# Halved patch loads with a matrix step between them, in a four-layer convolution network on one Trainium2 core

## The chip, the core and the metric

The kernel runs on one core of a Trainium2 chip. A core has TensorE (PE, matrix products into PSUM), VectorE (DVE), ScalarE (ACT), GpSimd (POOL) and SyncE (SP), which here does nothing but issue DMAs; sixteen DMA engines move data between HBM and SBUF. The metric is the device time of one execution in microseconds (us), the median of a few runs.

## What is computed

x is 16 images of 64 x 64 positions and 256 channels in float32, and everything stays float32. Four layers follow each other, each as x = x + f(groupnorm(x)) with 32 groups:

```
layer 0: linear attention with 8 heads over the 4096 positions, out projection, layer norm
layer 1: channel gate, two maps (mean, max over channels), 7x7 convolution of them -> fac,
         a state scan over the 4096 positions (16 states) added to fac,
         x * gate * fac, then batch norm over all 16 images, relu
layer 2: involution 3x3: per position 16 x 9 weights from a small network, applied to a projection
layer 3: involution 7x7: per position 16 x 49 weights from a small network, applied to groupnorm(x)
```

The batch norm of layer 1 needs a mean and a variance per channel over all images, so all of x1 * fac has to be seen once before its first value can be used.

## The kernel before

`network` is one program of four stages, with DRAM tensors between them: `x1_d` (layer 0's result), `fac_d` (fac, one row of 512 positions for each image and eighth of an image), `x2_d`, `x3_d` and `c3_d` (layers 1 and 2), and `strips` (layer 2's result, centred, cut in strips of 14 columns for the 7x7 patches, four quarters of 64 channels).

**Scan** (lines 631 to 780). For every eighth of the positions (`ch`) and each half of the images (`g`), `rowed` transposes the three rows of each of the 16 images (delta, delta times m squared, delta times m) to 48 partitions of `rows` (L726, L731). `decayed` (L733) makes two products of 48 partitions by 512 positions (L736), one for the decay, with an exponential on ACT (L740), and one for the input. A scan instruction on DVE follows (L749), four small products (L760), and two small DVE instructions (L767, L768). `ch` by `g` are 16 steps, written out in the text's order. At the end fac is transposed to `held`, and stored to `fac_d` (L779).

**Statistics** (L784 to L836). For each of 16 images and 8 eighths, a tile of x1 (512 KB, four buffers) is loaded (L789), PE spreads the row of `held` over the partitions (L792), DVE forms (x1 − mean) * fac with its sum (L797), ACT its squares with their sum (L801); then small DVE instructions make `bnp` and `ab`, the batch norm's factors.

**Layer 2** (L896 on) starts with its constants (L912 to L918: 5 loads, and 10 small ones in `folded`, L849). It is a pipeline of 152 turns, written out under `tc.manual_schedule()`: an image's eighth passes `end_of_layer1` (L960: the product again, L970, relu on ACT, L976, the sum on POOL, L980, and squares, L987), 13 turns later `projected`, from 21 on the involution, and 32 turns later `centred`. `loads(n + 1)` issues a turn's loads one turn ahead; `load_layer1` (L947) loads x1 and a spread copy of fac.

**Layer 3** (L1282 on). A turn is two bands of three rows of one quarter (64 channels) of one image: 16 x 4 x 11 = 704 turns. `load_patches` (L1404) loads a turn's patches `xw`, two DMAs of 128 partitions by 2 KB, six buffers, four turns ahead. `involution7` (L1433) multiplies them with the position's weight matrices, 32 products of 126 partitions, 32 columns and 48 elements (L1442), into a PSUM tile `pa`, from which ACT (L1454), DVE (L1455) and POOL (L1462, with the residual `rx`) make the output. Beside this, `matrices` (L1358) makes the weight matrices `wm` of the next quarter, in 24 steps; a step is four products on 64-row halves (L1376) into one of three PSUM tiles, then four ACT instructions (L1386) or one on DVE (L1391). `STEPS` spreads them: 3, 2, 2, 3, 2, 3, 2, 2, 3, 2 and 0 steps after the products of turns 0 to 10. Every third or fourth turn has a part of the next image's `reduced` (L1343). The last image's strips are made here, in eight units that borrow buffers of `xw` (L1515 to L1529).

The order of an engine's instructions is the text's inside `tc.manual_schedule()`, which holds for the scan and layer 2; elsewhere, layer 3 included, a scheduler may move them. All DMAs are issued by SP, in order, on eight semaphores in rotation: a DMA waits until the one eight before it has landed. A pool's tile waits for the release of the tile that had the buffer before. Every float32 product is two weight loads and two matmul records on PE.

The lines of layer 3's loop that the prediction needs:

```python
            if n + 4 < len(turns):
                pats.append(load_patches(*turns[n + 4]))
            ...
            involution7(i, quarter, t, wms[i, quarter], msk, pats.pop(0), ex[:, t % 2], rx[:, t % 2])
            ...
            for _ in range(STEPS[t]):
                next(making, None)
```

Of the kernel before, what the change touches and what calls it, by code (L numbers as in the profile page):

```python
# [15 lines left out]
P = 128  # L16
# [20 lines left out]
def network(ctx: ExitStack, tc: tile.TileContext, a: dict, out: bass.AP):  # L37
# [593 lines left out]
    with ExitStack() as st:  # L631
# [4 lines left out]
        sm = st.enter_context(tc.tile_pool(name="s_sm", bufs=2, space=PSUM))  # L636

# [6 lines left out]
        bng = sconst("bng", [P, 2], a["bn_gamma"])  # L644
        bnb = sconst("bnb", [P, 2], a["bn_beta"])
# [4 lines left out]
        wrow = sconst("wrow", [3 * NI, NG, 2, P], a["wrow"].rearrange("k (g n s) -> k g n s", g=NG, n=2))  # L650
        wout = sconst("wout", [P, 16], a["wstate"])
        mv2 = sconst("mv2", [P, 2, 2, NI])
# [56 lines left out]
        r3 = sconst("r3", [P, NB, NI, 3])  # L709
        rd, rdmm, rdm = (r3[:, :, :, k].rearrange("p d i -> p i d") for k in range(3))  # L710
        nc.vector.scalar_tensor_tensor(rd, z, 0.0, az, ALU.max, ALU.add)
        nc.vector.tensor_tensor(rdm, rd, m, ALU.mult)
        nc.vector.tensor_tensor(rdmm, rdm, m, ALU.mult)
# [5 lines left out]
        with tc.manual_schedule():  # L719
# [3 lines left out]
            def rowed(ch):  # L723
                pr = tr.tile([P, CT], F32, tag="tr", name="pr")
                for q in range(4):
                    nc.tensor.transpose(  # L726
                        pr[0 : 3 * NI, q * P : (q + 1) * P],
                        r3[:, ch * 4 + q].rearrange("p i k -> p (i k)"), ident,
                    )
                rows[ch] = wk.tile([3 * NI, CT], F32, tag="rows", name="rows", bufs=2)  # L730
                nc.scalar.copy(rows[ch], pr[0 : 3 * NI, :])  # L731

            def decayed(ch, g):  # L733
                pa = mm.tile([P, 2, CT], F32, tag="mm", name="pa")
                for k in range(2):
                    nc.tensor.matmul(  # L736
                        pa[:, k], lhsT=wrow[:, g, k, :], rhs=rows[ch], start=True, stop=True
                    )
                da = wk.tile([P, CT], F32, tag="da", name="da")
                nc.scalar.activation(da, pa[:, 0], AF.Exp)  # L740
                ins[ch, g] = da, pa
# [38 lines left out]
        facr = fac_d.rearrange("(i c) t -> i (c t)", i=NI)  # L780
# [3 lines left out]
        tot = sconst("tot", [P, 2, 2, NI, NCH])  # L784
        for i in range(NI):
            for ch in range(NCH):
                tk = slice(ch * CT, (ch + 1) * CT)
                x1 = wk.tile([P, 2, CT], F32, tag="x1", name="x1", bufs=4)
                nc.sync.dma_start(out=x1, in_=x1_d[i, :, :, tk].rearrange("h p t -> p h t"))  # L789
                pf = tr.tile([P, CT], F32, tag="tr", name="pf")  # L790
                row = i * NCH + ch
                nc.tensor.matmul(  # L792
                    pf, lhsT=ident[0:n, row : row + 1].broadcast_to([n, P]), rhs=held[0:n],
                    start=True, stop=True,
                )
                for h in range(2):
                    nc.vector.scalar_tensor_tensor(  # L797
                        x1[:, h], x1[:, h], ngm1[:, i, h : h + 1], pf, ALU.add, ALU.mult,
                        accum_out=tot[:, 0, h, i, ch : ch + 1],
                    )  # L800
                    nc.scalar.activation(  # L801
                        x1[:, h], x1[:, h], AF.Square, accum_out=tot[:, 1, h, i, ch : ch + 1]
                    )
        for k in range(2):
            nc.vector.tensor_reduce(mv2[:, :, k, :], tot[:, k], AX.X, ALU.add)
        nc.vector.tensor_scalar(mv2, mv2, 1.0 / NT, None, ALU.mult)
        sqm = sconst("sqm", [P, 2, NI])
        nc.vector.tensor_tensor(sqm, mv2[:, :, 0, :], mv2[:, :, 0, :], ALU.mult)
        nc.vector.tensor_tensor(mv2[:, :, 1, :], mv2[:, :, 1, :], sqm, ALU.subtract)
        for h in range(2):  # L810
            gate = ab[:, 0, :, h]
            nc.vector.tensor_tensor(mv2[:, h, 0], mv2[:, h, 0], gate, ALU.mult)
            nc.vector.tensor_tensor(mv2[:, h, 1], mv2[:, h, 1], gate, ALU.mult)
            nc.vector.tensor_tensor(mv2[:, h, 1], mv2[:, h, 1], gate, ALU.mult)


        mvb = sconst("mvb", [P, 2, 2])
        nc.vector.tensor_reduce(mvb[:, 0, :], mv2[:, :, 0, :], AX.X, ALU.add)
        nc.vector.tensor_scalar(mvb[:, 0, :], mvb[:, 0, :], 1.0 / NI, None, ALU.mult)
        dev = mv2[:, :, 0, :]  # L820
        for h in range(2):
            nc.vector.tensor_scalar(dev[:, h], dev[:, h], mvb[:, 0, h : h + 1], None, ALU.subtract)
        nc.vector.tensor_tensor(dev, dev, dev, ALU.mult)
        nc.vector.tensor_tensor(dev, dev, mv2[:, :, 1, :], ALU.add)
        nc.vector.tensor_reduce(mvb[:, 1, :], dev, AX.X, ALU.add)
        nc.vector.tensor_scalar(mvb[:, 1, :], mvb[:, 1, :], 1.0 / NI, None, ALU.mult)
        inv_sqrt(bnp[:, 0, :], mvb[:, 1, :], BN1_EPS)
        nc.vector.tensor_tensor(bnp[:, 0, :], bnp[:, 0, :], bng, ALU.mult)
        nc.vector.tensor_tensor(bnp[:, 1, :], mvb[:, 0, :], bnp[:, 0, :], ALU.mult)
        nc.vector.tensor_tensor(bnp[:, 1, :], bnb, bnp[:, 1, :], ALU.subtract)  # L830
        nc.vector.tensor_tensor(
            ab.rearrange("p t i h -> p (t i) h"),
            ab.rearrange("p t i h -> p (t i) h"),
            bnp[:, 0, :].unsqueeze(1).broadcast_to([P, 2 * NI, 2]),
            ALU.mult,
        )  # L836

    maps_st.close()

# [35 lines left out]
    def centred_strips(i, u, xc, cen, mean):  # L875

        nc.gpsimd.tensor_tensor(
            cen.rearrange("p q t c -> p t q c"),
            xc.rearrange("p t (q c) -> p t q c", q=4),
            mean.rearrange("p (q c) -> p q c", q=4).unsqueeze(1).broadcast_to([P, 4, 4, 64]),  # L880
# [4 lines left out]
        for w, dt in copies:  # L885
            for th in range(2):
                t0, t1 = max(0, th * 4 + dt), min(NTC, th * 4 + 4 + dt)
                s0 = t0 - th * 4 - dt
                parts.append((
                    strips[i, :, 3 : 3 + HW, w, t0:t1, :].rearrange("q r t c -> r q (t c)"),  # L890
                    cen[th:P:2, :, s0 : s0 + t1 - t0, :].rearrange("p q t c -> p q (t c)"),
                ))
# [3 lines left out]
    with ExitStack() as st:  # L896
# [20 lines left out]
        nc.sync.dma_start(out=ws[64:65, :], in_=a["bs"])  # L917
        sb2 = folded(pc, "l2", "L2_mean", "L2_var", "L2_gamma", "L2_beta", "br")  # L918
# [14 lines left out]
        loaded, stores, begun = [], [], []  # L933

# [25 lines left out]
        def end_of_layer1(i, rc):  # L960
# [6 lines left out]
            x1, pf = taken("x1"), taken("pf")  # L967
            zs = [wk.tile([P, 2, 256], F32, tag="z", name="z", bufs=1), pf]
            for h, z in enumerate(zs):
                nc.vector.scalar_tensor_tensor(  # L970
                    z, x1[:, h], ngm1[:, i, h : h + 1], pf, ALU.add, ALU.mult
                )
# [216 lines left out]
        def loads(n):  # L1189
# [6 lines left out]
            if end:  # L1196
                load_layer1(*end)

        with tc.manual_schedule():
            loads(0)  # L1200
# [81 lines left out]
    with ExitStack() as st:  # L1282
# [121 lines left out]
        def load_patches(i, quarter, t):  # L1404

            xw = wk.tile([P, 2, NTC, 64], F32, tag="xw", name="xw", bufs=6)
            rows = strips[i, quarter].rearrange("r w t c -> (r w) (t c)")
            for k in range(2):
                t0 = (t + k * NTT) * TR * (TC + 6)
                nc.sync.dma_start(  # L1410
                    out=xw[:, k].rearrange("p t c -> p (t c)"), in_=rows[t0 : t0 + P]
                )
# [20 lines left out]
        def involution7(i, quarter, t, wm, msk, xw, ex, rx):  # L1433


            pa = sm.tile([P, CT], F32, tag="sm", name="pa")
            pav = pa[:, 0 : 2 * TR * HW].rearrange("c (g a w) -> c (g a) w", g=2, w=HW)
            for tj in range(NTC):
                for k in range(2):
                    for q in range(2):  # L1440
# [5 lines left out]
                            lhsT=xw[0:TILE_IN, k, tj, 32 * q : 32 * q + 32],  # L1446
# [4 lines left out]
                        )  # L1451
            pag = pa[:, 0 : 2 * TR * HW].rearrange("c (g t) -> c g t", g=2)
# [23 lines left out]
        pats = [load_patches(*t) for t in turns[:4]]  # L1476
# [8 lines left out]
        gap = min(44, (4 * NTT * (NI - 1) - 4) // NCH)  # L1485
        for n, (i, quarter, t) in enumerate(turns):
# [21 lines left out]
            if n + 4 < len(turns):  # L1508
                pats.append(load_patches(*turns[n + 4]))
# [5 lines left out]
            if n % gap == 1 and n // gap < NCH:  # L1515
                xc = wk.tile([P, 4, C], F32, tag="xw", name="xc", bufs=6)
                nc.sync.dma_start(out=xc, in_=centred_from(NI - 1, n // gap))
# [8 lines left out]
            involution7(i, quarter, t, wms[i, quarter], msk, pats.pop(0), ex[:, t % 2], rx[:, t % 2])  # L1526
            if n % gap == 2 and n // gap < NCH:
# [130 lines left out]
```

## Time and profile before

| What | Value |
|---|---|
| three runs | 8206.47, 8218.75, 8226.33 us; median 8218.75 |
| profiled execution | 8218.71 us; span from first to last instruction 8216.8 us |
| instructions in the span | 213,294, of which PE 88,348 matmuls and as many weight loads |
| busy in the span | PE 83%, DVE 72%, ACT 59%, POOL 37% |
| DMA | 1695.53 MB, 206 GB/s on average |
| granted TensorE clock | 0.918 on average |
| layer 0 | 0 to 3053 us |
| scan, statistics | to 3174, to 3408 us |
| layer 2 | to about 5840 us |
| layer 3 | to 8214 us |

The profile shows one execution. An instruction group's line has its engine, line of the kernel, operation, tiles written and read and their shapes, and in square brackets how long the engine had been idle before it and which instruction ended the wait; "issue" means that no instruction or DMA of the profile ended it. PEld are weight loads, PE the matmuls. In the view by stretches each engine has its busy us and its count of instructions, and at the end stand the granted clock, the DMA engines' mean busy share and GB/s. DMA queue q1 carries the program's transfers, q8 and q14 carry instructions.

### The profile page before, as it was taken

How to read it: one execution, taken by the hardware profiler on the slowest of the kernel's cores; microseconds unless marked ns; L12 is line 12 of the kernel's file. 1: busy time of each engine (PE TensorE's matmuls, PEld its weight loads, DVE VectorE, ACT ScalarE, POOL GpSimd, SP SyncE). 2: the span in 40 equal slices, each digit the busy share in tenths (PEclk: the TensorE clock that was granted, in tenths of full speed). 3: DMA queues.
4: the chain of work that ended last, by engine and by line, in shares of the span. 5: the costliest groups of instructions: out<-in, count | busy, mean ns of one | idle time of the engine just before them, and what ended most of it. 6: DMA issues, size and time to landing. Idle time of an engine off the chain costs nothing. (4 is left out here: it accounts for less than half of the span.)

```text
span 8216.8 us, 213294 instructions
## 1 busy us (share of the span) xinstructions
PE 6831.6 (83%) x88348; PEld 5191.9 (63%) x88348; DVE 5933.2 (72%) x7071; ACT 4827.7 (59%) x11136; POOL 3044.1 (37%) x2154
## 2 busy tenths in 40 slices
PE   7888888888888867478888888888588888888897
PEld 5666666666666643156666666666477777777776
DVE  6787778787777775679999999999644444444444
ACT  3555555555555544676776767665455555555554
POOL 1222222222222210167888888887411212111112
PEclk9999999999999977798888888888799999999999
DMA  7644444344333334766777777775588888888887
GB/s 225 188 142 138 139 136 141 131 145 144 124 113 118 116 102 151 249 221 231 268 262 261 271 252 267 262 258 200 176 257 258 259 258 256 261 259 257 255 256 245
DMA packets 1079706, 1695.53 MB, mean 206 GB/s; under 512 B 136785, under 2 KB 682914, under 8 KB 1077586
## 3 DMA queue, kind: packets, MB, share of 16 engines
q1 hardware_dynamic: 1078738, 1681.89, 63.1%
q8 instruction: 696, 11.40, 0.6%
q14 instruction: 272, 2.23, 0.1%
HBM read 1234.54 MB, written 469.76 MB: 207 GB/s over the span
## 5 line engine op out<-in xcount | busy, mean ns | idle before, releaser
L1102 DVE TENSOR_TENSOR pd<-xs,pw 128x4608 f32<-128x4608 f32 x256 | 1261.2, 4946 | 1.4 <-ACT xs L1083 1.4
L1376 PE MATMUL pk<-rt,span 64*128 64x176 f32 x12288 | 1177.9, 328 | 52.6 <-issue 47.9
L1386 ACT ACTIVATE wm<-pk,spanb 128x176 f32<-128x176 f32 x2560 | 845.7, 424 | 573.4 <-PE pk L1376 570.3
L1115 POOL TENSOR_TENSOR pd<-pd 128x2048 f32<-128x2048 f32 (+2 forms) x384 | 1071.6, 2791 | 173.1 <-DVE pd L1102 82.7
L1462 POOL TENSOR_TENSOR ex<-ex,rx 128x192 f32<-128x192 f32 (+2 forms) x768 | 436.6, 570 | 1820.6 <-DVE ex L1455 1232.1
L1376 PEld LDWEIGHTS pk<-rt,span 64*128 64x128 f32 x12288 | 967.8, 191 | 132.8 <-issue 75.9
L1455 DVE SCALAR_TENSOR_TENSOR ex<-pa,msk,ex 128x192 f32<-128x192 f32 x704 | 294.3, 418 | 1006.5 <-ACT ex L1454 948.4
L292 PE MATMUL pkv<-wq,xn 128*128 128x256 f32 x4096 | 967.9, 382 | 14.4 <-ACT va L301 14.2
L1442 PE MATMUL pa<-wm,xw 126*32 126x48 f32 x45056 | 758.2, 214 | 220.9 <-issue 206.2
L375 POOL TENSOR_TENSOR qa<-qa,mq 128x1024 f32<-128x1024 f32 x256 | 507.4, 2005 | 1168.8 <-DVE mq L384 503.0
L1079 PE MATMUL pt<-ident,pad 128*128 128x128 f32 x4608 | 760.1, 327 | 214.8 <-ACT xs L1083 207.6
L1391 DVE TENSOR_TENSOR wm<-pk,spanb 128x704 f32<-128x704 f32 x896 | 794.2, 888 | 188.9 <-PE pk L1376 186.3
L292 PEld LDWEIGHTS pkv<-wq,xn 128*128 128x128 f32 x4096 | 771.3, 192 | 227.4 <-issue 101.1
L1442 PEld LDWEIGHTS pa<-wm,xw 126*32 126x32 f32 x45056 | 624.6, 111 | 403.1 <-issue 359.0
L1079 PEld LDWEIGHTS pt<-ident,pad 128*128 128x128 f32 x4608 | 623.6, 168 | 401.4 <-ACT xs L1083 265.5
L1083 ACT COPY xs<-pt 128x512 f32<-128x512 f32 x1152 | 608.0, 587 | 170.1 <-PE pt L1079 167.2
L1273 DVE TENSOR_REDUCE x<-pd 128x512 f32<-128x4608 f32 x128 | 634.0, 4953 | 4.4
L280 PE MATMUL pq<-xn,wq 128*128 128x512 f32 x1024 | 528.2, 631 | 91.2 <-DVE xn L166 74.0
L423 PE MATMUL py<-wo,o 128*128 128x256 f32 x2048 | 525.0, 412 | 31.4 <-DVE maps L510 27.6
L1454 ACT ACTIVATE ex<-pa,msk 128x192 f32<-128x192 f32 x704 | 299.2, 425 | 392.7 <-PE pa L1442 198.5
L423 PEld LDWEIGHTS py<-wo,o 128*128 128x128 f32 x2048 | 487.7, 310 | 63.9 <-issue 38.0
L1033 PE MATMUL px<-x2p,wis 128*128 128x512 f32 x1024 | 467.7, 599 | 12.8 <-DMA x2p<-x_d 8.1
(234 smaller groups left out, 11663.8 us busy)
## 6 DMA issues: line engine op xcount, KB each, us to landing
xw<-strips SPq DMA_DIRECT2D x1408, 256.0 KB
xn<-in_x SPq DMA_DIRECT2D x256, 512.0 KB
x_d<-x SPq DMA_DIRECT2D x256, 512.0 KB
strips<-cen SPq DMA_DIRECT2D x352, 256.0 KB
xin<-in_x SPq DMA_DIRECT2D x128, 512.0 KB
x<-in_x SPq DMA_DIRECT2D x128, 512.0 KB
xm<-x_d SPq DMA_DIRECT2D x128, 512.0 KB
x<-x_d SPq DMA_DIRECT2D x128, 512.0 KB
```

Source lines behind the costliest of these rows:

```text
L280: nc.tensor.matmul(pq, lhsT=wq[:, h, f0 : f0 + P], rhs=xn[:, h], start=(h == 0), stop=(h == 1),)
L292: nc.tensor.matmul(pkv[:, q], lhsT=xn[:, h, q * P : (q + 1) * P], rhs=wq[:, h, f0 + P : f0 + 384], start=(h == 0), stop=(h == 1),)
L423: nc.tensor.matmul(py[:, q, :], lhsT=om[i, hf][:, :, ch * 4 + q], rhs=wo[:, hf, :], start=(hf == 0), stop=(hf == 1),)
L1079: nc.tensor.transpose(pt[:, k, h * P : (h + 1) * P], lines[:, h, rc * 4 + e + k, 2 * j : 2 * j + P], ident,)
L1083: nc.scalar.copy(xs[:, e : e + 2, j, :], pt)
L1102: nc.vector.tensor_tensor(pd.rearrange("p r (g f) k -> p r g f k", f=16), run, pw.rearrange("p r (g k) -> p r g k", k=9).unsqueeze(3).broa ...
L1115: nc.gpsimd.tensor_tensor(pd[..., 0:n], pd[..., 0:n], pd[..., n : 2 * n], ALU.add)
L1273: nc.vector.tensor_reduce(x3[:, :, P:C], pd1, AX.X, ALU.add)
L1376: nc.tensor.matmul(pkv[:, b, m], lhsT=span[half, first + gg, s0 : s0 + P], rhs=rto[half, o // 4 * 2 + m, :], start=True, stop=True,)
L1386: nc.scalar.activation(dst[:, m // 2, m % 2], pkv[:, m // 2, m % 2], AF.Identity, bias=spanb[:, g0 + m : g0 + m + 1],)
L1391: nc.vector.tensor_tensor(dst, pkv, spanb[:, g0 : g0 + 4].rearrange("p (b m) -> p b m", b=2).unsqueeze(3).broadcast_to([P, 2, 2, NTL]), AL ...
L1442: nc.tensor.matmul(pav[p0 : p0 + 32, :, tj * TC : (tj + 1) * TC].rearrange("c g (w v) -> c g w v", v=2), lhsT=xw[0:TILE_IN, k, tj, 32 * q ...
```

## The change

Three parts, with the core of the diff.

**Scan in bands.** The transposed rows are laid out in four bands of 32 partitions: for each half of the images `g` one band with delta (8 rows) and one with the two others (16 rows). Each product of `decayed` takes only its band of `rows` and of `wrow`. `r3` lies in zeroed memory for that, and is written by six instructions.

```diff
+        r3 = pc.tile([P, NB, 2, 2, 32], F32, tag="r3", name="r3")
+        nc.gpsimd.memset(r3, 0.0)
...
-                rows[ch] = wk.tile([3 * NI, CT], F32, tag="rows", name="rows", bufs=2)
-                nc.scalar.copy(rows[ch], pr[0 : 3 * NI, :])
+                rows[ch] = wk.tile([P, CT], F32, tag="rows", name="rows", bufs=2)
+                nc.scalar.copy(rows[ch], pr)
...
                 for k in range(2):
+                    p0 = 64 * g + 32 * k
+                    band = slice(p0, p0 + 8 + 8 * k)
                     nc.tensor.matmul(
-                        pa[:, k], lhsT=wrow[:, g, k, :], rhs=rows[ch], start=True, stop=True
+                        pa[:, k], lhsT=wrow[band], rhs=rows[ch][band], start=True, stop=True
                     )
```

**Statistics within layer 2.** The loop and the small instructions after it move into `batch_norm`, called first inside layer 2's `manual_schedule`, so after layer 2's constants. `held` is read back from `fac_d`. x1 tiles alternate between two tags of three buffers, loaded five ahead. Images 1 to 15 come first; image 0 comes last, and its x1 and products stay in SBUF (in buffers that the involution uses later), where `end_of_layer1` takes them up for image 0.

```diff
+        def batch_norm():
...
+            nc.sync.dma_start(out=held, in_=fac_d)
+            todo = [(i, ch) for i in range(1, NI) for ch in range(NCH)]
+            todo += [(0, rc) for rc in range(NCH)]
...
+                if i:
+                    tag = ("x3", "x2r")[k % 2]
+                    x1 = wk.tile([P, 2, CT], F32, tag=tag, name="x1", bufs=3)
+                    tk = slice(ch * CT, (ch + 1) * CT)
+                    nc.sync.dma_start(out=x1, in_=x1_d[i, :, :, tk].rearrange("h p t -> p h t"))
+                else:
+                    x1 = kept[ch][0]
+                    for g in range(2):
+                        t0 = g * 2048 + ch * 256
+                        nc.sync.dma_start(
+                            out=x1[:, :, g * 256 : g * 256 + 256],
+                            in_=x1_d[i, :, :, t0 : t0 + 256].rearrange("h p t -> p h t"),
+                        )
...
+            if i:
+                x1, pf = taken("x1"), taken("pf")
...
+            else:
+                x1, zs = (t.rearrange("p h (g t) -> p h g t", g=2) for t in kept.pop(rc))
+                zs = [zs[:, h] for h in range(2)]
...
-            if end:
+            if end and end[0]:
                 load_layer1(*end)
...
         with tc.manual_schedule():
+            batch_norm()
             loads(0)
```

**Layer 3.** A turn's patches are two tiles, the left and the right four of the eight tile columns, each loaded by one DMA of 128 partitions by two rows of 1 KB, six buffers each, five turns ahead. The 32 products become `involved`, 16 for each half; after the first half one matrix step is made, the rest of the turn's steps after the second half. The turn loop stands in a `manual_schedule`. The last image's strips are made in 16 half units, in buffers of `xw0` and `xw1`.

```diff
+        def load_patches(i, quarter, t, part):
+
+            xw = wk.tile([P, 2, NTC // 2, 64], F32, tag=f"xw{part}", name="xw", bufs=6)
+            cols = strips[i, quarter].rearrange("r w t c -> (r w) (t c)")[
+                :, part * 256 : part * 256 + 256
+            ]
...
+            nc.sync.dma_start(out=xw.rearrange("p k t c -> p k (t c)"), in_=both)
...
-        gap = min(44, (4 * NTT * (NI - 1) - 4) // NCH)
+        gap = min(41, (4 * NTT * (NI - 1) - 4) // (2 * NCH))
+        in_order = ctx.enter_context(ExitStack())
+        in_order.enter_context(tc.manual_schedule())
...
-            involution7(i, quarter, t, wms[i, quarter], msk, pats.pop(0), ex[:, t % 2], rx[:, t % 2])
...
-            for _ in range(STEPS[t]):
+            pa = sm.tile([P, CT], F32, tag="sm", name="pa")
+            for part in range(2):
+                involved(t, wms[i, quarter], pa, part, pats[part].pop(0))
+                if n + 5 < len(turns):
+                    pats[part].append(load_patches(*turns[n + 5], part))
+                if part == 0 and STEPS[t]:
+                    next(making, None)
+            involution7(quarter, t, msk, pa, ex[:, t % 2], rx[:, t % 2])
...
+            for _ in range(STEPS[t] - 1):
                 next(making, None)
```

## The prediction

> **What bounds the kernel now.** I read the busy time of each engine by stage first, because a share over the whole span says nothing of four layers with different limits. The columns are stretch, its us, busy us of PE, PEld, DVE, ACT and POOL (instructions in brackets), granted clock, DMA share, GB/s.
>
> ```profile
> 3053.00:3174.00 121.00, 105.87 (x252) 55.24 (x250) 39.11 (x76) 21.93 (x33) 0.00 (x0) 0.54 0.00 0
> 3174.00:3408.50 234.50, 156.55 (x256) 41.65 (x256) 180.82 (x514) 177.21 (x513) 0.00 (x0) 0.93 0.85 279
> 3408.50:3468.40 59.90, 0.00 (x0) 0.00 (x0) 18.87 (x48) 24.29 (x60) 28.74 (x19) 0.50 0.67 185
> 3468.40:5840.00 2371.60, 1967.99 (x10592) 1425.01 (x10592) 2269.82 (x1276) 1612.44 (x3604) 1857.32 (x892) 0.88 0.73 248
> 5945.00:8214.00 2269.00, 1973.82 (x58644) 1669.48 (x58642) 1050.83 (x1644) 1262.56 (x3720) 455.31 (x776) 0.97 0.83 256
> ```
>
> In order these are the scan, the statistics, layer 2's first eight turns (image 0), the rest of layer 2 (VectorE 96% busy; the change hardly touches it) and layer 3. The scan has PE 87% busy at a granted clock of 0.54, with no DMA. The statistics have no full engine, and DMA at 0.85. The eight turns have nothing full. Layer 3 has PE at 87% and DMA at 0.83.
>
> The timeline then shows how each works. First one step of the scan, then its end:
>
> ```profile
> 3085.44 3.78 PE L736 MATMUL pa<-rows,wrow 48*128 48x512 f32 x4
> 3089.15 1.89 PE L760 MATMUL pys<-wout,hst 128*128 128x16 f32 x8
> 3090.88 1.03 PE L726 MATMUL pr<-ident,r 128*48 128x128 f32 x4
> ```
>
> PE goes straight from one to the next: it is the scan's path. The four records of L736 start 0.85 us apart.
>
> In the statistics the DMA queue's own waits show who holds the loads, and for layer 3 the timeline shows a turn without a pause and one with:
>
> ```profile
> SPq L789 <- ACT x L801: 170.9, 124, 3.9
> ```
>
> ```profile
> 6607.14 1.00 PE L1442 MATMUL pa<-wm,xw 126*32 126x48 f32 x64
> 6608.07 1.46 PE L1376 MATMUL pk<-rt,span 64*128 64x176 f32 x16
> 6609.47 0.99 PE L1442 MATMUL pa<-wm,xw 126*32 126x48 f32 x64
> ```
>
> ```profile
> 6597.79 0.45 PE L1442 MATMUL pa<-wm,xw 126*32 126x48 f32 x18
> ...
> 6601.44 0.48 PE L1442 MATMUL pa<-wm,xw 126*32 126x48 f32 x10 [3.19 <-issue]
> ```
>
> A smooth turn with two matrix steps takes 2.33 us; the mean is 2269/704 = 3.22. The pauses are "issue": nothing that the profile knows. The DMA view of the same stretch names a candidate:
>
> ```profile
> q1 hardware_dynamic: 379412, 572.96, 81.2%
> q8 instruction: 460, 7.54, 1.4%
> ```
>
> 460 fetches of 16 KB for 117,300 PE instructions is one per 256. I counted the trace's PE records in pages of 256 from the start of the program: the pauses sit at one and the same position in the page from 0 to 8214 us. No page starts sooner than 2.19 us after its fetch's packet started. In layer 3, 298 of 458 pages begin after a pause over 0.25 us, 338 us in all. A page takes 4.93 us on average, 4.19 of it execution. Layer 3 is paced by its code: after a pause the next fetch starts 2.35 us later on average (5% to 95%: 1.3 to 3.5), plus 2.2, so about 4.55 us go by before another page can begin.
>
> **The change part by part.** The sum is made against the profiled execution, 8218.71 us (span 8216.8 and 1.9 around it); the median of the three runs is 8218.75, the same.
>
> *Scan in bands.* L736's two products now contract over partitions 0 to 15 of two different 32-row bands instead of all 48 rows. The near row is L1376, whose products on two 64-row halves start in pairs 7 ns apart, every pair 147 ns. So the four records should start in two slots rather than four: 2 x 0.85 = 1.7 us less in each of 16 steps, 27 us. What is late next: the scan on VectorE and its two small products, 1.27 + 2 x 0.21 with about 2 us of L760, still less than PE's step. The transposes now load 128 columns instead of 48, r3 is written in six half-size instructions for three (+0.3 us), and bands and full array alternate; I take 2 us off. −25 us; between −27 and 0 if the bands don't overlap. The memset of r3 costs about 3.5 us on POOL (4096 elements by L923's 7.58 us for 8976) at a time when POOL is empty, before 3065.5, when it is first needed.
>
> *Statistics in layer 2.* Removed ahead of them: four x1 tiles loaded during the scan. Added: fac_d's store must land, and is then loaded again as held. In the changed program's order SP issues layer 2's 17 constants between the two; 15 of them took 3413.07 to 3423.31 before, so about 11 us with bng and bnb. x1's loads stand behind them. Store 2.5 (estimate from other landings here) + 11 + 0.4 = about 14 us before the first load; before, DVE began 2.1 us after the store. Against it stands the pace. Before, the loads were issued every 1.81 us (3178.7 to 3401.1), and SP waited 171 us for ACT to release one of four buffers; now there are six. The next limit is DVE at 2 x 0.67 = 1.34 us a tile, and DMA before that: at a share of 0.95 instead of 0.85, 1.81 x 0.85/0.95 = 1.62. Stretches of 10 us in layer 2 show shares about 1.0, so 0.95 is within reach. 14 + 128 x 1.62 + 6 (last load to last square, 7.2 before) = 227 against 234: −7 us. Ends: pace 1.81 gives +19, pace 1.45 gives −28.
>
> *Image 0 kept.* Turns 0 to 7 lose their loads and the two products of L970. They took 60 us from the end of the statistics to turn 8, with 15 constants queued ahead of turn 1. Left are the moments (4.6 us), then ACT's four passes of 0.9 us a turn, POOL's 2 x 1.27 beside them: 8 x 3.7 = 30, and about 2.5 until turn 8's load, issued only one turn ahead, is there. 37 instead of 60: −23 (−15 to −27).
>
> *Layer 3, halves.* Two extra changes of shape per turn in 630 of 704 turns (t = 10 and the last quarter have no steps). By the trace's starts, L1442 to L1376 takes 0.138 us, L1376 to L1442 0.239, and within a run the next record starts after 0.012 and 0.04. So +0.32 us of PE per turn, 204 us in all, or +0.44 per page: execution 4.63 instead of 4.19. What hides it is the wait for code. Of the pages, those that execute 4.0 to 4.5 us take 4.76 in all, those of 4.5 to 5.0 take 5.10; at 4.63 that is about 5.0, against 4.93: 460 x 0.07 = +32 us. The gain is in the mixture: pages that ran in 2.5 to 3.5 us waited over 1 us, and with a step in every half they become rare.
>
> [...]
>
> *Loads by halves.* Again two issues a turn of 256 KB each, now 256 rows of 1 KB. SP pays about 0.04 us more for such a shape (x1 0.46 beside pf 0.43); it is 87% in issue here, and the cover is five turns of loads. 1 KB packets took 46 ns at the median, 2 KB 84: 92 for 84. [...] After a pause the fetch started 2.32 us later at shares of 0.78 to 0.86 and 2.63 at 0.86 to 0.92, which speaks for about +0.06; it started 2.42 later at 147 to 182 packets a us and 2.23 above 182, which speaks for −0.1 with smaller packets. I take −0.04 a page, −18 us; bounds −0.25 to +0.12, −115 to +55.
>
> *Order of the text, prefetch, image 15's strips by halves.* The PE order before already was turn, steps, turn; six buffers hold six turns in both. Where a half-strip takes a slot of xw0 or xw1, the next patch load on SP waits until PE has done that half of the turn under way; residual loads and stores of that turn stand behind it, but all are for turns two to five ahead. Taken at 0, bounds ±10.
>
> Sum: −25 −7 −23 +32 −18 = −41, about 8178.
>
> **Rivals.**
> A. As summed, 8178 (8150 to 8208): 0.47.
> B. Fetches wait less behind 1 KB packets, or the even mixture pays more: 0.2 us less per page than summed, 460 x 0.2 = −92, so 8086 (8050 to 8120). For: the fetch's start at high packet rates. Against: bytes per engine are the same. 0.20.
> C. Slower: the drains show. At the changes between L1442 and L1376, 0.32 us a turn, if execution and not code paces a page, which starts once a page executes longer than its fetch takes, about 4.6 us; exactly there it stands by my sum. Half of the 204 shown, less the 55 ahead of it: 8266 (8235 to 8330). 0.20.
> D. The edits ahead of layer 2 don't do what they say: bands in sequence (0), pace 1.81 (+19), turns −15; with +14 in layer 3, 8237 (8220 to 8255). 0.13.
>
> **How the numbers follow.** ±0.2% (16 us) is about what a measurement can tell from no change. Faster: A 0.42 + B 0.20 = 0.62. Same: A 0.05, C 0.02, D 0.06 = 0.13. Slower: C 0.18, D 0.07 = 0.25. The range 8075 to 8262 leaves out part of B and about half of C.
>
> **What would show it.** Scan: starts of L736's successor in pairs, stage about 96 us. Statistics: a bubble of about 14 us, then loads every 1.6. Turn 8 some 37 us after the last square. Layer 3 some 14 us longer, with fewer than today's 152 pauses of over 1 us, and a page near 4.96. The prediction is wrong if the fetch's own delay moves by more than 0.1 us, since that is multiplied by 460.

## The result and the profile after

The changed kernel takes 8214.25 us (median of 12 runs, 8201.65 to 8228.12), the kernel before 8220.69 us beside it (12 runs). The ratio is 0.9994 with a 95% interval of 0.9984 to 1.0004: nothing that can be told from no change, where 0.5% less was forecast. The profiled execution of the changed kernel took 8215.72 us (span 8213.9). In the code after the change the lines are: L742 the scan's products (L736 before), L957 and L962 the statistics on VectorE and ACT (L797, L801), L1034 the start of `end_of_layer1` (L970), L1444 the matrix steps (L1376), L1510 the involution's products (L1442).

The view by stretches of the changed kernel, with the same columns as in the prediction. The rows are the scan, the wait between the store of fac and the first product of the statistics, the statistics, image 0's eight turns, the rest of layer 2, and layer 3:

```profile
3062.00:3161.00 99.00, 78.70 (x249) 46.27 (x248) 40.19 (x82) 21.98 (x33) 0.00 (x0) 0.55 0.00 0
3161.00:3178.00 17.00, 1.56 (x2) 0.84 (x3) 1.91 (x8) 0.25 (x1) 8.13 (x2) 0.50 0.33 98
3178.00:3354.00 176.00, 143.65 (x271) 41.53 (x269) 172.92 (x514) 172.31 (x512) 0.00 (x0) 0.98 1.02 378
3354.00:3385.60 31.60, 0.00 (x0) 0.00 (x0) 3.71 (x24) 23.52 (x60) 20.61 (x17) 0.50 0.41 147
3385.60:5760.00 2374.40, 1972.78 (x10592) 1428.27 (x10592) 2267.33 (x1276) 1613.87 (x3604) 1856.41 (x892) 0.88 0.73 247
5864.00:8210.00 2346.00, 2128.31 (x58650) 1683.52 (x58650) 1075.08 (x1646) 1263.98 (x3721) 459.87 (x784) 0.97 0.83 248
```

So the change does do something: two large effects of opposite sign meet. From the last start of L505, where layer 0 ends, to layer 3's first involution product it took 2890.7 us before and 2801.9 now: 89 us gained. Layer 3, from its first involution product to its last, took 2267.2 us before and takes 2344.2 now: 77 us lost. Layer 0, which the change does not touch, ended at 3053.7 us before and at 3062.1 now. Over all profiles of this study it ended between 3049 and 3067, so a difference of 10 us between two single profiles can't be placed.

One step of the scan, from the timeline of the changed kernel:

```profile
3103.32 2.08 PE L742 MATMUL pa<-rows,wrow 8*128 8x512 f32 x4
3105.32 1.89 PE L766 MATMUL pys<-wout,hst 128*128 128x16 f32 x8
3107.05 1.09 PE L730 MATMUL pr<-ident,r 128*128 128x128 f32 x4
```

The four records of L742 take 2.08 us where L736 took 3.78; by the trace they start in two pairs, 7 ns apart within a pair and 1.0 us from pair to pair. In the statistics the DMA queue's wait for ACT is this (171 us before):

```profile
SPq L927 <- ACT x L962: 106.2, 114, 2.8
```

Layer 3's timeline shows the products in halves (x32), with a matrix step (x8) after each:

```profile
7001.72 0.58 PE L1510 MATMUL pa<-wm,xw 126*32 126x48 f32 x32
7002.24 0.87 PE L1444 MATMUL pk<-rt,span 64*128 64x176 f32 x8
7003.04 0.58 PE L1510 MATMUL pa<-wm,xw 126*32 126x48 f32 x32
7003.54 0.87 PE L1444 MATMUL pk<-rt,span 64*128 64x176 f32 x8
```

The DMA view of layer 3, with packets, MB and share of the sixteen engines:

```profile
q1 hardware_dynamic: 563018, 573.32, 81.4%
q8 instruction: 461, 7.55, 1.4%
```

The bytes, the engines' share and the fetches of code are about as before (572.96 MB, 81.2%, 460 fetches); the packets rose from 379,412 to 563,018.

### The profile page after: what moved, and what is told of

Its sections match the earlier page's. It is cut to its first block, busy times and chain, and to the rows that moved or that the text cites. A ratio compares the mean times of both kernels' runs of the same rounds, so it can differ in the third digit from the quotient of the medians.

```text
span 8213.9 us, 214052 instructions
## 1 busy us (share of the span) xinstructions
PE 6964.5 (85%) x88364; PEld 5208.7 (63%) x88364; DVE 5929.2 (72%) x7058; ACT 4825.1 (59%) x11136; POOL 3052.3 (37%) x2163
## 3 DMA queue, kind: packets, MB, share of 16 engines
q14 instruction: 279, 2.28, 0.1%
## 5 line engine op out<-in xcount | busy, mean ns | idle before, releaser
L1444 PE MATMUL pk<-rt,span 64*128 64x176 f32 x12288 | 1300.1, 336 | 17.6 <-issue 14.6
L1444 PEld LDWEIGHTS pk<-rt,span 64*128 64x128 f32 x12288 | 948.2, 190 | 122.2 <-issue 22.5
L1510 PE MATMUL pa<-wm,xw 126*32 126x48 f32 x45056 | 864.9, 216 | 133.1 <-issue 98.2
L1510 PEld LDWEIGHTS pa<-wm,xw 126*32 126x32 f32 x45056 | 654.4, 112 | 433.3 <-issue 335.2
```

The lines of the kernel that those rows point to most:

```text
L1444: nc.tensor.matmul(pkv[:, b, m], lhsT=span[half, first + gg, s0 : s0 + P], rhs=rto[half, o // 4 * 2 + m, :], start=True, stop=True,)
L1510: nc.tensor.matmul(pav[p0 : p0 + 32, :, tj * TC : (tj + 1) * TC].rearrange("c g (w v) -> c g w v", v=2), lhsT=xw[0:TILE_IN, k, tj % (NTC / ...
```

## The experiments

The table has layer 3 as counted from each kernel's trace, with the same counting of pages of 256 PE instructions as in the prediction: a page's execution (its whole time less the pause at the page's start, so other waits are inside it), its whole time, the sum of the pauses at the pages' starts, and how long after a page's start the next fetch starts when a pause lay before it. The ratio is to the kernel before, measured beside each. Kernels of different groups ran on different chips, so ratios are compared, not times. Each trace is a single execution, and by the scatter of its pages a mean in the last column has a standard error of about 0.05 us.

| Kernel | ratio (95%) | execution / page, us | pauses, us | fetch starts after, us |
|---|---|---|---|---|
| before | 1 | 4.19 / 4.93 | 338 | 2.35 |
| changed | 0.9994 (0.9984-1.0004) | 4.72 / 5.09 | 170 | 2.26 |
| head_only | 0.9891 (0.9867-0.9914) | 4.27 / 4.95 | 316 | 2.30 |
| l3_only | 1.0105 (1.0086-1.0124) | 4.76 / 5.17 | 187 | 2.42 |
| whole_in_order | 0.9908 (0.9893-0.9923) | 4.32 / 4.99 | 305 | 2.35 |
| halves_scheduled | 0.9976 (0.9967-0.9984) | 4.63 / 5.10 | 215 | 2.36 |
| halves_together | 0.9968 (0.9955-0.9981) | 4.35 / 5.10 | 343 | 2.39 |
| step_between_whole | 0.9943 (0.9925-0.9961) | 4.73 / 5.05 | 146 | 2.24 |
| packets_1k | 0.9966 (0.9952-0.9979) | 4.37 / 5.14 | 351 | 2.49 |
| half_loads | 0.9677 (0.9653-0.9702) | 4.17 / 4.61 | 201 | 2.06 |
| switches_doubled | 1.0286 (1.0271-1.0301) | 5.57 / 5.63 | 28 | 1.83 (22 pauses) |
| switches_halved | 0.9924 (0.9909-0.9939) | 4.35 / 5.04 | 316 | 2.17 |
| order_mended | 0.9987 (0.9977-0.9996) | 4.63 / 5.06 | 196 | 2.33 |
| whole_mended | 0.9880 (0.9860-0.9899) | 4.22 / 4.90 | 311 | 2.30 |

All kernels but before and l3_only have the changed head (the scan in bands, the statistics in layer 2). three_buffers and held_first, below, have layer 3 as before.

### The two parts, and halves against order

**head_only**: the changed kernel with layer 3's loop of before.

```diff
-            xw = wk.tile([P, 2, NTC // 2, 64], F32, tag=f"xw{part}", name="xw", bufs=6)
+            xw = wk.tile([P, 2, NTC, 64], F32, tag="xw", name="xw", bufs=6)
...
-            for part in range(2):
-                involved(t, wms[i, quarter], pa, part, pats[part].pop(0))
...
+            involution7(i, quarter, t, wms[i, quarter], msk, pats.pop(0), ex[:, t % 2], rx[:, t % 2])
```

> The scan and the statistics as changed, layer 3 as before (patches whole, all steps after the products, scheduler free). The profiles say that the changed kernel reaches layer 3 about 80 us sooner (first product of layer 3 at 5863.5 against 5944.0 us) and loses 77 us in it. If the two halves of the change don't touch each other, layer 3 takes its 2269 us again and the time is about 8140, ratio 0.990. Rival: layer 3's loss comes from what lies ahead of it (another position of its code in the pages, data left in another state); then layer 3 stays near 2345 us and the time near 8214.

Measured 8151.21 us, 0.9891. The head alone gains 1.1%, about 90 us.

**l3_only**: the kernel before with layer 3's loop of the changed one, the mirror image of the diff above.

> The scan and the statistics as before, layer 3 as changed. If the parts add up: 8220 + 77 = about 8297, ratio 1.009, layer 3 near 2345 us with a page near 5.09 us. If layer 3's loss hangs on the part ahead of it: about 8220.

Measured 8325.62 us, 1.0105. 0.9891 x 1.0105 = 0.9995: within the intervals the two parts multiply to the change, so neither loss nor gain needs the other part.

**whole_in_order**: head_only with the order of the text in layer 3.

```diff
+        in_order = ctx.enter_context(ExitStack())
+        in_order.enter_context(tc.manual_schedule())
         for n, (i, quarter, t) in enumerate(turns):
```

> Head as changed; layer 3 as before, but its turn loop in the order of the text. Theory S (the changes of shape are not hidden; order costs nothing, as the prediction took it): same as with the old layer 3 and the scheduler, about 8140, layer 3 near 2270 us. Theory O (order of the text: at each image's change PE waits 2.1 us for VectorE's two small products of the reduced weights, and some 2 us in other places, about 65 us in all): 8140 + 40 to 65 = 8180 to 8205, layer 3 2310 to 2335 us. Theory L (1 KB packets hold the fetches up): about 8140.

**halves_scheduled**: the changed kernel without these two lines.

> The changed kernel with the order of the text lifted in layer 3: the scheduler may move instructions, halves and the step between stay. Theory S: about 8214, layer 3 near 2345 us. Theory O: 40 to 65 us less, 8150 to 8175, layer 3 2280 to 2305 us. Theory L: about 8214.

Measured 0.9908 and 0.9976. With whole and halved patches, with the scheduler and in the order of the text, the four kernels form a square. Halving costs 0.85% with the scheduler (0.9891 to 0.9976) and 0.86% in the text's order (0.9908 to 0.9994), about 70 us. The order costs 0.17% and 0.18%, about 14 us, less sure than the other, since the intervals of a pair touch or overlap. Theory O, the order alone, is out: the halves are most of the loss.

### Halves: the loads, or the step between

**halves_together** keeps the loads by halves and makes all steps after both halves' products; **step_between_whole** loads the patches whole and keeps the step between. Beside whole_in_order (neither) and the changed kernel (both) they complete a second square.

```diff
# halves_together
-                if part == 0 and STEPS[t]:
-                    next(making, None)
...
-            for _ in range(STEPS[t] - 1):
+            for _ in range(STEPS[t]):
# step_between_whole
-            xw = wk.tile([P, 2, NTC // 2, 64], F32, tag=f"xw{part}", name="xw", bufs=6)
+            xw = wk.tile([P, 2, NTC, 64], F32, tag="xw", name="xw", bufs=6)
...
-                involved(t, wms[i, quarter], pa, part, pats[part].pop(0))
+                involved(t, wms[i, quarter], pa, part, xw)
```

> Head and order of the text as changed, patches loaded in halves of 1 KB rows, but both halves' products together and all steps after them. Beside it stands the run with whole patches in the order of the text (0.9908). Theory S (the 0.86% between that run and the changed kernel is the changes of shape): stays at 0.991 +- 0.002, layer 3 near 2290 us. Theory L (it is the loads: 1 KB packets, the fetches behind them): 0.999. The prediction's own term for the packets, -18 us, would give 0.989.

> The mirror image: patches whole, 2 KB rows, four turns ahead, but one matrix step between the left and the right half of a turn's products, order of the text. Theory S: 0.999 +- 0.002, layer 3 near 2345 us. Theory L: 0.991. If both matter, half-way: 0.995.

Measured 0.9968 and 0.9943: the loads cost 0.60% (49 us), the step between 0.35% (29 us), each give or take some 0.2%. Theory S fell as stated; both matter, and the loads more. In step_between_whole a page executes 4.73 us instead of 4.32, which is about 190 us of PE over 459 pages, and 29 us of it show: pauses fell from 305 to 146 us. The same can be read from the chief wait of PE in layer 3 (total us, times, longest), in whole_in_order and in step_between_whole:

```profile
PE pa L1510 <- issue: 187.1, 188, 2.8
```

```profile
PE pa L1508 <- issue: 81.1, 103, 2.6
```

That is the cover that the prediction named, and it hid most of the cost.

**packets_1k** puts the loads' cost to the test alone: whole tile, same buffers, same place in SP's order, two DMAs a turn, but each takes half of the columns of both bands.

```diff
-            for k in range(2):
-                t0 = (t + k * NTT) * TR * (TC + 6)
-                nc.sync.dma_start(
-                    out=xw[:, k].rearrange("p t c -> p (t c)"), in_=rows[t0 : t0 + P]
-                )
+            for part in range(2):
+                cols = rows[t0 : t0 + P, part * 256 : part * 256 + 256]
...
+                nc.sync.dma_start(
+                    out=xw.rearrange("p k t c -> p k (t c)")[:, :, part * 256 : part * 256 + 256],
+                    in_=both,
+                )
```

> The kernel with whole patches in the order of the text (0.9908) with one edit: a turn's two loads fill the same tile at the same place in the program, but each takes the left or the right half of both bands (256 rows of 1 KB) instead of one band (128 rows of 2 KB). Theory P (the 0.60% between that kernel and the one with halves loaded and used together is the packets: fetches of code start later among twice as many): 0.9968, fetch 2.22 us or more after a page's start against 2.16. Theory Q (it is the half tiles: their loads stand behind the products in SP's order and five turns ahead, SP waited 315 us for PE there against 180, and loads behind it come late): 0.991.

Measured 0.9966, within 0.0002 of halves_together. Buffers, depth of the prefetch and place in SP's queue are cleared: the split into 1 KB packets is enough to make the loss. The DMA view of layer 3, whole_in_order and then packets_1k:

```profile
q1 hardware_dynamic: 379639, 573.29, 81.1%
```

```profile
q1 hardware_dynamic: 557975, 572.95, 81.1%
```

The bytes are the same and the packets 47% more; the engines have the same share of a stage that is 3% longer. PE's waits in layer 3 that nothing in the profile ends, for products and for matrix steps, are 187.1 us (the line above) and 46.1 in whole_in_order; in packets_1k both are longer:

```profile
PE pk L1444 <- issue: 46.1, 51, 2.6
```

```profile
PE pa L1517 <- issue: 211.9, 206, 3.1
PE pk L1444 <- issue: 56.9, 49, 3.3
```

Waits for the patches did not become large (2.1 us in all). After a pause the fetch starts 0.14 us later than in whole_in_order, but in halves_together only 0.04, which is within the error. Taken over all pages, with or without a pause, the difference is steadier: 2.15 us after the page's start in whole_in_order, 2.27 in packets_1k, 2.25 in halves_together (each ±0.04), and, in the pair with the step between, 1.96 in step_between_whole and 2.12 in the changed kernel. From a fetch's start to the start of its page after a pause it takes 2.5 us on average in all five. So it is the start that is late, not the fetch that is slow. Taking each page with the pause that follows it, pages that execute 3.5 to 4.0 us took 4.66 us in whole_in_order and 4.86 in packets_1k, those of 4.0 to 4.5 us 4.80 and 4.92. One thing stays open: over whole runs the mean granted clock was 0.9163 in packets_1k and 0.9185 in whole_in_order. Whether the pauses lower it or something else does is not shown, so part of the loss may come by way of the clock.

**half_loads** asks whether fetches queue behind the kernel's own packets at all. It leaves out the loads of every second turn and uses the patches of the turn before once more, so its output is not the network's.

```diff
-            if n + 4 < len(turns):
-                pats.append(load_patches(*turns[n + 4]))
+            if n + 4 < len(turns) and n % 2 == 0:
+                pats += [load_patches(*turns[n + 4])] * 2
```

> The kernel with whole patches in the order of the text, but a turn of an odd place uses the patches of the turn before it: half of the patch loads are left out (the output is that of repeated patches). Traffic in layer 3 falls from 254 to about 170 GB/s, PE's work stays. If a fetch's 2.2 us of delay are queueing behind the kernel's own packets, they fall, the pauses of 305 us mostly go, and layer 3 takes about 2290 - 250 = 2040 us, ratio 0.961. If the delay is a fetch's own, the pauses stay and the ratio is 0.988 to 0.991.

Measured 0.9677, nearer to the first case. Layer 3 in the view by stretches, and its DMA queue:

```profile
5855.00:7971.00 2116.00, 1906.98 (x58617) 1633.27 (x58615) 1048.97 (x1647) 1260.77 (x3722) 455.51 (x774) 0.98 0.63 188
```

```profile
q1 hardware_dynamic: 278672, 389.83, 61.8%
```

PE has as many instructions as in whole_in_order, in a stage 175 us shorter. Of these 175 us, 104 are pauses, which fall from 305 to 201 us. Another 44 or so are waits of PE for loads of c3, in whole_in_order and then here; those are not waits for code:

```profile
PE pr L1411 <- DMA c<-c_d: 58.9, 33, 4.7
```

```profile
PE pr L1411 <- DMA c<-c_d: 14.4, 10, 3.9
```

After a pause the fetch starts 2.06 us after the page's start instead of 2.35. The pauses don't vanish: the other part of the delay is the fetch's own, or belongs to the traffic that stays. Fewer issues by SP go with fewer packets here; in packets_1k the number of issues is the same, and the delay moved all the same (2.15 to 2.27 us over all pages).

### When changes of shape show

**switches_doubled** splits further, **switches_halved** makes five steps after every second turn.

```diff
# switches_doubled
+                        if m == 0:
+                            yield
...
+                for half in range(2):
+                    tj = part * 4 + half * 2
+                    involved(t, wms[i, quarter], pa, range(tj, tj + 2), xw)
+                    if (part, half) != (1, 1) and STEPS[t]:
+                        next(making, None)
# switches_halved, on head_only
-        STEPS = (3, 2, 2, 3, 2, 3, 2, 2, 3, 2, 0)
+        STEPS = (0, 5, 0, 5, 0, 5, 0, 5, 0, 4, 0)
```

> The changed kernel with more changes of shape: a turn's products in four quarters, half a matrix step (two products) after each of the first three, the rest after the fourth; PE's program then has 3077 changes between the two kinds where the changed kernel has 2371 and the kernel before 1237 (counted over products in the program, where turns without steps share one). The changes are some 0.15 us each beyond what a record costs within a run: 706 x 2 / 2 x 0.15 = about 106 us more of PE. If PE's execution now sets the pace of nearly every page: 80 to 106 us more, 1.009 to 1.012. If waits for code still hide most of it, as the prediction reckoned (0.16 shown of each us): 20 to 40 us, 1.002 to 1.004.

> Head as changed, layer 3 as before with the scheduler, but the steps only after every second turn (0, 5, 0, 5, ... steps): 759 changes of shape where the kernel with the old layer 3 has 1237 (0.9891), so 478 x 0.15 = 72 us less of PE. If the changes of shape cost their full time here too: 0.981 (layer 3 near 2205 us). If below 4.5 us of execution a page the code sets the pace: at most 20 us, 0.987 to 0.990; with pages of uneven mixture (runs of products fetch-bound, runs of steps PE-bound) it can be slower than 0.9891.

Doubled: 1.0286. The count in the expectation, 3077, was too low: by the trace the changes between involution products and matrix steps are some 4900, against 2400 in the changed kernel. With that count the price fits: a page executes 5.57 instead of 4.72 us, 459 x 0.85 = about 390 us, over some 2500 more changes 0.16 us each. Of these 390 us, 2.92% or 240 us show, 61%, where the first doubling, from whole_in_order to step_between_whole, showed 15%. The reason stands in the wait that had covered them (this is all that is left of it):

```profile
PE pa L1512 <- issue: 13.2, 15, 2.3
```

Pauses are 28 us in all, where the changed kernel has 170: what could be hidden is used up. In the changed kernel's trace the pause that follows a page is 0.64 us on average if the page executed less than 4.5 us, and 0.15 us if it executed more than 5 us. So the cover runs out somewhere between the two, gradually.

Halved: 0.9924, slower than head_only (0.9891). It does not test the price downwards, for the execution of a page did not fall (4.35 against 4.27): in runs of five steps PE waits for ACT to empty `pk`,

```profile
PE pk L1444 <- ACT wm L1454: 28.9, 131, 1.1
```

and pauses over 2 us are 54 where head_only has about 30.

### The order's share

**order_mended** and **whole_mended** put layer 3's small work earlier in the text, in the changed kernel and in whole_in_order.

```diff
+            if n % (4 * NTT) == 4 * NTT - 2 and i + 1 < NI:
+                masks.append(mask(i + 1))
+            if n + 6 in features and features[n + 6][0] == 0:
+                weigh(features[n + 6][1])
+            if n + 5 in features and features[n + 5][0] == 0:
+                weigh_mean(features[n + 5][1])
...
-            if n + 2 in features:
-                cs[features[n + 2]] = load_reduced(*features[n + 2])
+            if n + 3 in features:
+                cs[features[n + 3]] = load_reduced(*features[n + 3])
```

> The changed kernel, with the small work of layer 3 put earlier in the text: an image's reduced weights are made on VectorE six turns ahead and used on PE five turns ahead, its mask two turns ahead, c3 is loaded three turns ahead instead of two. PE's waits for these (31 + 31 + about 12 us in the changed kernel's trace) should be gone. If such waits show in full: 0.9994 - 0.0075 = 0.992. If they are the order's cost as measured (the scheduler's version stands at 0.9976): 0.9976. If pauses for code take their place: 0.9994.

> The same with whole patches in the order of the text (0.9908; its trace has 59 us of waits for c3, 19 us for the weights). If the waits show in full: 0.9815. If they are the order's cost as measured (the scheduler's version stands at 0.9891): 0.989. If pauses take their place: 0.991.

Measured 0.9987 and 0.9880. Two of PE's waits in the changed kernel's layer 3 (total us, times, longest) belong to this small work: for loads of c3, and, once for each image, for VectorE's reduced weights, which stand behind a matrix step in VectorE's order:

```profile
PE pr L1411 <- DMA c<-c_d: 31.6, 24, 3.7
PE pm L1396 <- DVE wr L1390: 30.4, 15, 2.9
```

In order_mended the second line is gone; the first stays at 31.9 us, so loading c3 one turn earlier moved nothing. Pages execute some 40 us less in all; pauses rise by 26. The gain, 0.07% and 0.28%, is in both pairs small enough for the intervals to overlap. The order costs little, and its waits partly take the place of pauses; how its 0.17% divides stays open. whole_mended, the changed head with whole patches, is the fastest kernel here that computes the network: 8117.56 us, 1.2% below before. head_only, at 0.9891, can't be told from it.

### The statistics

**three_buffers** gives the x1 tiles one tag of three buffers; **held_first** reads `held` back ahead of layer 2's constants. Both have layer 3 as before.

```diff
# three_buffers
-                    tag = ("x3", "x2r")[k % 2]
+                    tag = ("x3", "x3")[k % 2]
```

> Changed head, layer 3 as before (0.9891), but the x1 tiles of the statistics share one tag of three buffers instead of two tags of three. The pace went from 1.81 us a tile with four buffers (before) to 1.37 with six, where the prediction had 1.62. If the buffers decide it: three buffers give 1.81 x 4/3 = 2.4 us a tile at most, at least 1.81, so 120 x 0.44 to 1.0 = 53 to 120 us more, ratio 0.9955 to 1.0035. If something else that changed in the statistics does (held read back, no store beside it, loads after the constants): stays near 1.37 and 0.989.

> Changed head, layer 3 as before (0.9891), and held is read back ahead of layer 2's 17 constants instead of behind them. In the changed kernel the wait of VectorE between the store of fac and the first product of the statistics is 17 us, of which SP's constants are 12. If the first x1 loads are what waits, they still stand behind the constants and nothing is gained (0.989); if held's own landing is what ends last (PE began 0.0 us after it, the x1 tile had about as long), at most 1 to 2 us. A gain of 10 us would need both ahead.

Measured 1.0030 and 0.9894. held_first gains nothing, as expected: the x1 loads still stand behind the constants. In three_buffers the statistics' products run from 3173 to 3446 us, 273 for 120 tiles, 2.28 us a tile. The wait for a buffer, and the stretch:

```profile
SPq L927 <- ACT x L962: 214.1, 117, 2.9
```

```profile
3173.00:3446.00 273.00, 190.60 (x247) 51.03 (x245) 169.80 (x477) 165.31 (x476) 0.00 (x0) 0.74 0.76 231
```

Three buffers give 2.28 us a tile, four gave 1.81, six 1.36 (161.7 us for 119 tiles). Pace times buffers is 6.8, 7.2 and 8.2 us: a buffer's round trip is about 7 us, and with three or four buffers the pace is that trip divided by their number. By that division six would allow 1.2, and VectorE's own 1.35 a tile (172.92 us for 128 tiles) takes over: it is 98% busy in that stretch. With three and four buffers DMA was not the limit (shares 0.76 and 0.85, at 231 and 279 GB/s where 378 was reached with six); with six its share is 1.02, so it is about as full as VectorE, though SP still waits 106 us for a buffer.

## Why the prediction was wrong, step by step

- *Scan in bands, −25*: nearly right. From the first to the last scan instruction 92.9 us became 68.9, −24, with the starts in pairs. The first scan instruction comes 2.6 us later after the end of layer 0, so the stage as a whole, to the store of fac, gained 21.
- *Statistics, −7*: the bubble was nearly right (17 us from the store of fac to the first product, 2 before). The pace was not: "DMA before that: at a share of 0.95 instead of 0.85, 1.81 x 0.85/0.95 = 1.62". That scaled bytes by the engines' share. The stretch after the change has a share of 1.02 and 378 GB/s, where 0.85 had gone with 279: the share rose by a fifth and the bytes by 35%. What set the pace was the number of buffers. From the store to the last square it took 192.5 us instead of the 227 forecast, 34 us better.
- *Image 0 kept, −23*: right in kind, −28 (60 to 31.8 us from the last square to turn 8).
- *Layer 3, halves, +32*: right. The step between costs 0.35% or 29 us, give or take some 16. Its execution (+0.41 us a page for +0.44) and its cover were as reckoned. In whole_in_order the pauses at the pages' starts are 305 us; step_between_whole, which adds PE work, has 146, and half_loads, with a third of the bytes and no work of PE taken away, 201.
- *Loads by halves, "I take −0.04 a page, −18 us"*: this step failed. It is +0.60%, +49 us or about +0.11 us a page, inside its bounds but near the upper one (+55). The prediction added two readings of one trace, +0.06 for fuller engines and −0.1 for more packets a us, and the second had the wrong sign: with the packets alone changed, the fetch starts about 0.1 us later, not earlier. Readings within one kernel show what goes together. Whether packets per us rise there with PE's mixture of work, and whether this made the −0.1, is not shown. No run shows the +0.06 either: the share of layer 3 was 81.1% in packets_1k as in whole_in_order, and 81.4% in the changed kernel, so the engines did not become fuller. The transfers themselves took little longer (92 ns for two packets of 1 KB against 84 for one of 2 KB, at the median in layer 3 of the kernel before), and PE waited for patches 2.1 us in all in packets_1k; the loss does not lie there.
- *Order of the text, 0 within ±10*: about +14, not settled in its parts.

Put together from the runs: −90 for the head, +29, +49 and +14 make +2; −5 to −6 was measured, and the steps are each known to some 15 us. Of the forecast's 41 us, the packets took 67 (+49 instead of −18) and the order 14, and the head gave back 35 more than summed. That the total came out so near to zero is two misses that cancel, not a merit of the sum.

8214 lies in the range of none of the four rivals: A ends at 8208, D begins at 8220. Rival C foresaw a loss in layer 3, but from the changes between products and matrix steps alone (0.32 us a turn). Most of that time was still hidden at 4.73 us a page, in step_between_whole, where 15% of it showed; in switches_doubled, which executes 5.57 us a page, 61% does show, as C's reasoning has it. B, faster fetches behind 1 KB packets, is refuted by packets_1k (2.27 us after a page's start against 2.15), and D by the stretches of the head.

## What to carry over

Where pauses at the pages' starts take as much of a stage as here (305 of 2291 us in whole_in_order), count its DMA packets as well as its bytes: splitting transfers that PE hardly waited for (2.1 us in packets_1k) cost 49 us, and the fetches started 2.27 us after a page's start instead of 2.15. Of the work added to PE in this stage 15% showed where a page's execution went from 4.32 to 4.73 us, and 61% where it went from 4.72 to 5.57. The prediction's estimate of the fetch's period, 4.55 us from 2.35 and 2.2 in the kernel before, lies below both 4.73 and 5.57: compare execution and period before counting on the cover. In the statistics the pace was a buffer's round trip (about 7 us) divided by the number of buffers, 2.28 and 1.81 us a tile with three and four, until VectorE's own 1.35 was reached; work that out before scaling a DMA share.

## What the runs showed of the hardware that was not expected

- With 573 MB and a share of 81.1% unchanged, 47% more packets made the kernel 0.58% longer; with a third of the bytes gone (188 GB/s instead of 254) a fetch started 0.29 us sooner after a pause. So in packets_1k bytes and share alone did not tell when a fetch starts: 2.27 us after the page's start, against 2.15 in whole_in_order.
- In the statistics a 2 KB packet took 99 ns on average in the kernel before (279 GB/s) and 87 ns in the changed one (378 GB/s), with a median of 84 in both. So a share of 0.85 was not 85% of what the engines could move.
- Layer 0, whose text is the same in all kernels here, ended between 3049 and 3067 us in their profiles.
